# A mixture-of-experts kernel on Trainium2: the third row tile of each expert cut from 384 to 352 rows, with a branch at the end for the rows left out, and the last transfer freed of a wait

## The chip, the cores and the metric

The kernel runs on one core of a Trainium2 chip. The core has a matrix engine (PE, whose weight loads are shown apart as PEld), a vector engine (DVE), an activation engine (ACT), a general engine (POOL) and a queue engine (SP), each with an instruction stream of its own; they meet at semaphores. Transfers are started by SP, or by POOL where rows are scattered through a list of indices. The metric is the time of one execution on the device in microseconds, and lower is better.

## The reference

The input x has 8 sequences of 512 tokens with 256 features. Two layers follow each other, both with a residual: a causal attention with 16 heads whose context passes a convolution of width 3 and then attends again, and a block of attention with rotary embedding followed by a mixture of experts. The change concerns the mixture of experts. For the 4096 tokens (normalized rows `xf`) it computes

```python
probs = softmax(xf @ w_router)                 # 8 experts
topw, topi = top_k(probs, 2)                   # each token goes to two of them
combine = sum(one_hot(topi, 8) * (topw / sum(topw))[..., None], axis=1)
g = silu(einsum('td,xdh->txh', xf, wg))        # 256 -> 704, each expert
u = einsum('td,xdh->txh', xf, wu)
eo = einsum('txh,xhd->txd', g * u, wd)         # 704 -> 256
out = einsum('txd,tx->td', eo, combine)
```

All arithmetic is in f32. There are 4096 x 2 = 8192 pairs of a token and an expert, a mean of 1024 for each expert. How many an expert gets depends on the input.

## The kernel before

`block_kernel` calls `fast_path` and then, under a branch on the count `few`, `general_path`. The fast path assumes some bounds on its inputs, `sums_in_range` and `count` test them in the run itself, and the general path, which computes everything again without them, runs only where a test failed. In the traced run it is jumped over (L619).

The fast path has two stages. In the first, up to about 880 us, two attentions at a time go through a schedule written out turn by turn (`plan`, `units`). `route` picks the two experts of every token, and `slots` gives each pair a place in the table `xtab` in device memory. Expert `e` owns the `CAP` = 1152 rows from `e * CAP` on. `run` counts the places given so far and `limit` is the end of each expert's part. A row of the table holds the 256 features of the token, its number, and its eight weights. Rows that no token fills keep the padding that `fill` wrote at the start. Their token number lies outside the output, so that a transfer to it is dropped.

In the second stage every expert goes through its 1152 rows as three tiles of N = ET * P = 384. Of the 24 tiles, (0, 0) runs ahead, inside the end of the first stage; `places` lists the others: (0, 1), then experts 1 to 7 with their tiles 0 to 2, then (0, 2). `expert_tile` is a generator, and the loop at L1970 steps two tiles in turn, so that a tile's steps stand in this order on every engine:

- `load_rows` (L726, on SP) fetches the rows of the tile after next. Three buffers `xg` take turns, so a load waits until the scatters of the tile three before it have landed. `load_expert` (L711) fetches the weights of the next expert into one of two sets of buffers.
- Six transposes on PE (L744) and two scalings on ACT (L747) make `xgT`, with the features on the partitions. They stand ahead of the second product of the tile before.
- `up` (L755): for each of six blocks `k` of the hidden width the products with `wg` and `wu`, with the expert's weights stationary and the tile's 384 rows moving. ACT applies silu (L769, L772) and DVE multiplies (L770, L773) into `hT`. The last block is half as wide, and its two products share one.
- L780: for each `s` of three groups of 128 rows, six products with `hT` stationary and the 256 columns of `dn` (`wd`) moving. DVE multiplies by the token's weight for this expert into `share` (L787), and POOL scatters the rows of `share` with addition into `out` (L792).

The order on PE, ACT, DVE and POOL is the order in which the program issues (`manual_schedule`); only SP's is the framework's. In PSUM, `pgu` and `po` have two buffers each.

The scatters add to rows of `out` that others may also add to. `unordered` states what has to wait. Within a tile all rows are different, so its first two transfers wait only for the last transfer of the tile before (`added`) and for those that stored the residual (`stored`); the third also waits for the first two, so that to wait for it means to wait for all:

```python
for i in sent[:-1]:
    if last:
        tc.add_manual_dep(sent[-1], i.name, data, reason="the last one")
    else:
        tc.declare_no_dep(sent[-1], i, reason="rows of their own")
```

At n = 2 in the loop `sums_in_range` reduces the tests to a column `good` on DVE (L810 to L825), at n = 3 `count` sums it over the partitions with one product (L831) and writes `few` (L833). Every engine loads `few` at the end of its stream (L1986; SP earlier) and compares (L619). L2031 stands for the program's closing: SP waits for every semaphore, POOL drains, and the engines meet.

Of the kernel before, what the change touches and what calls it, by code (L numbers as in the profile page):

```python
# [11 lines left out]
F32 = mybir.dt.float32  # L12
I32 = mybir.dt.int32
AF = mybir.ActivationFunctionType
ALU = mybir.AluOpType
AX = mybir.AxisListType
PSUM = bass.MemoryType.PSUM

P = 128
B, S, D = 8, 512, 256  # L20
# [5 lines left out]
DC = D // P  # L26
# [11 lines left out]
NB = S // KB  # L38
LARGE = 1e20
ET = 3  # L40
CAP = 3 * ET * P
ROW = D + 1 + NE


# [566 lines left out]
@with_exitstack  # L611
def block_kernel(
    ctx: ExitStack,
    tc: tile.TileContext,
    *args: bass.AP,
):
    few = fast_path(tc, *args)

    with tc.If(few < P):  # L619
        general_path(tc, *args)  # L620


@with_exitstack
def fast_path(
    ctx: ExitStack,
    tc: tile.TileContext,
    x: bass.AP,
    wqkvT: bass.AP,
    bqkv: bass.AP,
# [49 lines left out]
            nc.sync.dma_start(xs[b], x[b * S : (b + 1) * S, :].rearrange("(c p) d -> p c d", p=P))  # L679


    dram = ctx.enter_context(tc.tile_pool(name="dram", bufs=1, space=bass.MemoryType.DRAM))
    xtab = dram.tile([NE * CAP, ROW], F32, tag="xtab", name="xtab")

    run = keep.tile([P, NE], F32, tag="run", name="run")
# [25 lines left out]
    def load_expert(e, gu, dn):  # L711
# [9 lines left out]
        nc.gpsimd.memset(dn[:TAIL, HT, :], 0.0)  # L721
        return e, gu, dn

    def load_rows(xg, e, i):
        r0 = e * CAP + i * N
        nc.sync.dma_start(xg, xtab[r0 : r0 + N, :].rearrange("(p s) w -> p s w", s=ET))  # L726
        return xg

    def token_of(xg, s):
        return bass.IndirectOffsetOnAxis(ap=xg[:, s, D : D + 1].bitcast(I32), axis=0)  # L730

    added = []

    stored = []

    def expert_tile(expert, xg, room):


        e, gu, dn = expert
        xgT = room("xgT")  # L740
        for d in range(DC):
            pt = room("pt")
            for s in range(ET):
                nc.tensor.transpose(  # L744
                    pt[:, s * P : (s + 1) * P], xg[:, s, d * P : (d + 1) * P], ident
                )
            nc.scalar.mul(xgT[:, d, :], pt, g2_sb[:, d : d + 1])  # L747
        yield
        hT = room("hT")
        nc.gpsimd.memset(hT[HT][:TAIL], 0.0)  # L750
        yield

        def up(ps, n0):
            for d in range(DC):
                nc.tensor.matmul(  # L755
                    ps,
                    gu[d][:, n0 : n0 + P],
                    xgT[:, d, :],
                    start=(d == 0),
                    stop=(d == DC - 1),  # L760
                )

        for k in range(NK):
            pg, pu = room("pgu")
            up(pg, k * P)
            sg = room("sg")
            if k < HT:
                up(pu, UP + k * P)
                nc.scalar.activation(sg, pg, AF.Silu)  # L769
                nc.vector.tensor_mul(hT[k], sg, pu)  # L770
            else:
                nc.scalar.activation(sg[TAIL:P, :], pg[:TAIL, :], AF.Silu)  # L772
                nc.vector.tensor_mul(hT[k][TAIL:P, :], sg[TAIL:P, :], pg[TAIL:P, :])  # L773
            yield
        sent = []
        share = room("share")
        for s in range(ET):
            po = room("po")
            for k in range(NK):
                nc.tensor.matmul(  # L780
                    po,
                    hT[k][:, s * P : (s + 1) * P],
                    dn[:, k, :],
                    start=(k == 0),
                    stop=(k == NK - 1),
                )
            nc.vector.tensor_scalar(  # L787
                share[:, s, :], po, xg[:, s, D + 1 + e : D + 2 + e], None, ALU.mult
            )

            sent.append(
                nc.gpsimd.indirect_dma_start(  # L792
                    out=out,
                    out_offset=token_of(xg, s),
                    in_=share[:, s, :],
                    in_offset=None,
                    bounds_check=B * S - 1,
                    oob_is_err=False,
                    compute_op=ALU.add,
                ).ins  # L800
            )
            unordered(sent, added[-1:] + stored, s == ET - 1)
            if s == ET - 1:
                added[:] = sent[-1:]
            yield


    def sums_in_range():
        good = keep.tile([P, 4], F32, tag="good", name="good")
        nc.vector.tensor_reduce(good[:, 0:2], total, AX.X, ALU.add)  # L810
        nc.vector.tensor_scalar(good[:, 0:2], good[:, 0:2], LARGE, None, ALU.is_lt)

        nc.vector.tensor_mul(good[:, 0:1], good[:, 0:1], turns[:, 1:2])
        nc.vector.tensor_mul(good[:, 1:2], good[:, 1:2], turns[:, 0:1])
        nc.vector.tensor_add(good[:, 0:1], good[:, 0:1], good[:, 1:2])
        nc.vector.tensor_reduce(good[:, 1:2], rtotal, AX.X, ALU.add)
        nc.vector.tensor_scalar(good[:, 1:2], good[:, 1:2], LARGE, None, ALU.is_lt)
        nc.vector.tensor_mul(good[:, 2:3], good[:, 0:1], good[:, 1:2])
        nc.vector.tensor_tensor(limit, run, limit, ALU.is_le)
        nc.vector.tensor_reduce(good[:, 3:4], limit, AX.X, ALU.min)  # L820
        nc.vector.tensor_mul(good[:, 2:3], good[:, 2:3], good[:, 3:4])

        nc.vector.tensor_tensor(early, early, needed, ALU.is_ge)
        nc.vector.tensor_reduce(good[:, 3:4], early, AX.X, ALU.min)
        nc.vector.tensor_mul(good[:, 2:3], good[:, 2:3], good[:, 3:4])  # L825
        return good

    def count(good, pc):
        all_one = keep.tile([P, 1], F32, tag="all_one", name="all_one")
        nc.vector.memset(all_one, 1.0)  # L830
        nc.tensor.matmul(pc[0:1, 0:1], good[:, 2:3], all_one, start=True, stop=True)  # L831
        few = keep.tile([1, 1], I32, tag="few", name="few")
        nc.vector.tensor_copy(few, pc[0:1, 0:1])  # L833
        return few

    with ExitStack() as att:
        wp = att.enter_context(tc.tile_pool(name="wp", bufs=1))
# [974 lines left out]
        with tc.manual_schedule(  # L1812
# [157 lines left out]
            for n, (e, i) in enumerate(places):  # L1970
                if i == 1 and n:
                    more = (e + 1) % NE
                    weights[more] = load_expert(more, *room("weights"))
                if n + 2 < len(places):
                    rows[n + 2] = load_rows(room("xg"), *places[n + 2])
                if n:
                    go_on(parts[n], 1 + NK)
                if n + 1 < len(places):
                    parts[n + 1] = expert_tile(weights[places[n + 1][0]], rows[n + 1], room)
                    go_on(parts[n + 1])  # L1980
                go_on(parts[n], ET)
                if n == 2:
                    good = sums_in_range()
                if n == 3:
                    few = count(good, room("po"))
    return nc.values_load(few, min_val=0, max_val=P)  # L1986


# [46 lines left out]
```

## Time and profile before

| | |
|---|---|
| three runs | 1419.48, 1420.53 (median), 1425.67 us |
| profiled execution | 1420.22 us |
| its span, from first to last instruction | 1418.5 us |
| granted PE clock, mean | 0.997 |
| expert products `pgu` (L755) | 1056 records, 345.8 us busy |
| second products `po` (L780) | 864 records, 190.6 us busy |
| scatters into `out` (L792) | 72, mean 1.555 us |
| first to last record of L755 | 848.2 to 1398.7 us |

The profile shows one execution. A product of f32 operands stands in it as two records, each with a weight load of its own: 22 products with `wg` and `wu` in a tile are 44 records, 18 with `wd` are 36. A transpose is one record. The records of PE overlap, so their mean duration (L755: 487 ns) is longer than the distance from one to the next, and a busy share near 100% only says that PE has no gap. What one more or one less record costs is read from the distances. The time of a run is longer than the span by what lies before the first instruction and after the last: 1.72 us in the profiled execution.

### The profile page before, as it was taken

The numbers are of one execution on the slowest core, as the hardware profiler recorded it, in microseconds if no ns is written. First come the engines' busy times: TensorE is split into PE (matmuls) and PEld (weight loads), VectorE is DVE, ScalarE is ACT, GpSimd is POOL, SyncE is SP. The second block draws the span as 40 slices with busy tenths as digits, with TensorE's granted clock in tenths as the row PEclk, the third lists the DMA queues.
The fourth block names the chain that finished last, engine by engine and source line by source line (L and its number), as shares of the span: only waits on it lengthen the run. The fifth ranks groups of instructions, "written<-read, shape, count | busy, mean of one in ns | idle before, by whom it ended". The sixth has DMA issues, their size and how long they took to land.

```text
span 1418.5 us, 31892 instructions
## 1 busy us (share of the span) xinstructions
PE 1375.9 (97%) x13476; PEld 893.0 (63%) x13476; DVE 740.7 (52%) x1466; ACT 725.4 (51%) x1175; POOL 526.5 (37%) x525
## 2 busy tenths in 40 slices
PE   8999999999999999999999999999999999999996
PEld 5566555566565665565565666676766767676674
DVE  5755887775977775976676855322121222222221
ACT  4777786776787775787776883211121111112110
POOL 3334333546334555434555344331212122221212
PEclk9999999999999999999999999999999999999998
DMA  5122122211001211011211022423232323232311
GB/s 150 59 85 86 62 81 77 77 43 54 13 32 46 88 43 43 13 56 43 86 64 67 24 79 88 115 46 95 32 94 39 90 43 89 38 90 64 69 22 14
DMA packets 65767, 88.68 MB, mean 63 GB/s; under 512 B 12880, under 2 KB 46096, under 8 KB 65616
## 3 DMA queue, kind: packets, MB, share of 16 engines
q1 hardware_dynamic: 52080, 69.21, 15.0%
q0 software_dynamic: 13536, 17.35, 7.0%
q8 instruction: 107, 1.75, 0.5%
q14 instruction: 44, 0.36, 0.1%
HBM read 36.62 MB, written 32.08 MB: 48 GB/s over the span
## 4 chain that ended last, share of the span: by engine, by line
PE 58%; DVE 5%; ACT 3%; issue 2%; DMA 1%; POOL 1%; POOLq 0%; DVEq 0%; ACTq 0%; SPq 0%
PE pgu L755 23%; PE po L780 12%; PE sc L1204 8%; PE av L1134 6%; PE mm L1044 4%; PE mm L1397 2%; ACT pr L1211 2%; PE mm L1033 1%; PE mm L1062 1%; DVE r L1164 1%; PE mm L744 1%; DVE c L1165 1%; PE mm L1286 1%; POOL out_dram L792 0%; DMA out_dram<-share,xg 0%
## 5 line engine op out<-in xcount | busy, mean ns | idle before, releaser
L1211 ACT ACTIVATE pr<-sc 128x1024 f32<-128x1024 f32 x432 | 418.7, 1023 | 143.8 <-PE sc L1204 141.4
L1219 POOL TENSOR_TENSOR pr<-pr,seen 128x512 f32<-128x512 f32 (+1 forms) x216 | 256.6, 1188 | 394.8 <-ACT pr L1211 385.5
L755 PE MATMUL pgu<-xgT,gu 128*128 128x384 f32 x1056 | 345.8, 487 | 2.2 <-DVE hT L770 1.6
L755 PEld LDWEIGHTS pgu<-xgT,gu 128*128 128x128 f32 x1056 | 200.0, 190 | 137.0 <-DVE hT L770 2.2
L769 ACT ACTIVATE sg<-pgu 128x384 f32<-128x384 f32 x120 | 58.8, 490 | 410.8 <-PE pgu L755 410.8
L792 POOL DMA_INDIRECT out_dram<-share,xg x72 | 112.0, 1555 | 385.8 <-DVE share L787 306.2
L1134 PE MATMUL av<-pr,va 64*32 64x64 f32 (+7 forms) x6144 | 218.8, 407 | 0.0
L770 DVE TENSOR_TENSOR hT<-sg,pgu 128x384 f32<-128x384 f32 x120 | 66.4, 554 | 247.2 <-ACT sg L769 247.2
L1204 PE MATMUL sc<-qT,kT 32*128 32x320 f32 (+7 forms) x2048 | 191.1, 434 | 4.3 <-ACT pr L1211 4.2
L780 PE MATMUL po<-dn,hT 128*128 128x256 f32 x864 | 190.6, 379 | 0.0
L1134 PEld LDWEIGHTS av<-pr,va 64*32 64x32 f32 x6144 | 113.1, 106 | 102.9 <-issue 73.9
L780 PEld LDWEIGHTS po<-dn,hT 128*128 128x128 f32 x864 | 162.4, 190 | 21.6
L1164 DVE RECIPROCAL r<-r 128x256 f32<-128x256 f32 x96 | 167.4, 1744 | 12.0 <-DMA r<-cs 11.9
L1204 PEld LDWEIGHTS sc<-qT,kT 32*128 32x128 f32 x2048 | 115.2, 184 | 77.5 <-ACT pr L1211 30.8
L787 DVE TENSOR_SCALAR share<-po,xg 128x256 f32<-128x256 f32 x72 | 34.8, 484 | 149.3 <-PE po L780 147.1
L1204 PE MATMUL sc<-q2T,kT 32*128 32x512 f32 (+7 forms) x1024 | 92.9, 434 | 0.6 <-ACT pr L1211 0.5
L1644 POOL DMA_INDIRECT xtab<-rows,slot x64 | 64.0, 1000 | 41.8 <-DVE pick L1633 26.3
L1204 PEld LDWEIGHTS sc<-q2T,kT 32*128 32x128 f32 x1024 | 58.3, 184 | 32.6 <-issue 14.7
L1044 PE MATMUL mm<-xT,wqkv_sb 128*128 128x512 f32 x128 | 62.7, 616 | 3.8 <-ACT mm L1539 2.3
L1044 PE MATMUL mm<-xaT,wqkv_sb 128*128 128x512 f32 x128 | 61.3, 612 | 2.0 <-DVE xaT L1292 2.0
L1397 PE MATMUL mm<-terms,conv_sb 128*128 128x256 f32 x256 | 62.7, 390 | 0.0
L1151 ACT ACTIVATE cs<-av 128x512 f32<-128x512 f32 x96 | 56.6, 603 | 4.5 <-PE av L1134 3.9
(177 smaller groups left out, 1302.5 us busy)
## 6 DMA issues: line engine op xcount, KB each, us to landing
r<-cs SPq DMA_DIRECT2D x96, 128.0 KB
xtab<-pad SPq DMA_DIRECT2D x24, 397.5 KB
xg<-xtab SPq DMA_DIRECT2D x24, 397.5 KB
gu<-in_wg_dram SPq DMA_DIRECT2D x18, 352.0 KB
cs<-cs SPq DMA_DIRECT2D x48, 128.0 KB
dn<-in_wd_dram SPq DMA_DIRECT2D x9, 640.0 KB
gu<-in_wu_dram SPq DMA_DIRECT2D x18, 320.0 KB
x<-in_x_dram SPq DMA_DIRECT2D x8, 512.0 KB
```

Of the source, the lines that this page charges most:

```text
L755: nc.tensor.matmul(ps, gu[d][:, n0 : n0 + P], xgT[:, d, :], start=(d == 0), stop=(d == DC - 1),)
L770: nc.vector.tensor_mul(hT[k], sg, pu)
L780: nc.tensor.matmul(po, hT[k][:, s * P : (s + 1) * P], dn[:, k, :], start=(k == 0), stop=(k == NK - 1),)
L792: nc.gpsimd.indirect_dma_start(out=out, out_offset=token_of(xg, s), in_=share[:, s, :], in_offset=None, bounds_check=B * S - 1, oob_is_err ...
L1044: nc.tensor.matmul(ps, w[:, d, n0 : n0 + P], srcT[:, d, :S], start=(d == 0), stop=(d == DC - 1),)
L1134: nc.tensor.matmul(av[i][g * HP : (g + 1) * HP, j * KB :], v[rows, j, ch * G + g, :], pr[rows, g, at : at + n], start=(j == 0), stop=(j == ...
L1164: nc.vector.reciprocal(r[:, half], r[:, half])
L1204: nc.tensor.matmul(sc[:, g - g0, at : at + S - j * KB], kT[r0 : r0 + HP, ch, j], qT[r0 : r0 + HP, ch, j * KB : S], start=True, stop=True,)
L1211: nc.scalar.activation(pr[:, g0 : g0 + 2], sc, AF.Exp, scale=SCALE)
L1219: nc.gpsimd.tensor_tensor(diag, diag, seen.unsqueeze(1).unsqueeze(1).to_broadcast([P, G, len(parts), KB]), ALU.mult,).ins
L1397: nc.tensor.matmul(ps[:, i], conv_sb[:, d, k, ch * P : (ch + 1) * P], self.terms[d][:, k], start=(d == 0), stop=(d == DC - 1),)
L1644: nc.gpsimd.indirect_dma_start(out=xtab, out_offset=bass.IndirectOffsetOnAxis(ap=slot[:, c, k : k + 1], axis=0), in_=rows[:, c, :], in_off ...
```

## The change

`MOST` = 1120 rows of each expert go through the fast path instead of `CAP` = 1152, so the tiles of an expert have 384, 384 and 352 rows; the table keeps its size. The third tile's rows are loaded in two transfers, 256 rows with two to a partition and 96 rows with one, where one transfer brought three to a partition. Its third group has 96 rows. The other tiles keep their shapes.

`rows_left` computes the last `FEW` = 32 rows of every expert from the table. It stands under a branch on a second count, which is 128 only if all tests hold with each `limit` lower by 32; `general_path` stands under a branch of its own inside that one. `sums_in_range` gets four more DVE operations, `count` returns two numbers (`held`), and the pools `dram` and `counts` are opened in `block_kernel`, around both.

The very last transfer of the last tile (`final`) is declared independent of the other two of its tile, where it waited for them.

```diff
@@ -38,7 +38,9 @@
 NB = S // KB
 LARGE = 1e20
 ET = 3
-CAP = 3 * ET * P
+FEW = 32
+MOST = 3 * ET * P - FEW
+CAP = MOST + FEW
 ROW = D + 1 + NE
 
 
@@ -614,16 +616,84 @@
     tc: tile.TileContext,
     *args: bass.AP,
 ):
-    few = fast_path(tc, *args)
-
-    with tc.If(few < P):
-        general_path(tc, *args)
+    dram = ctx.enter_context(tc.tile_pool(name="dram", bufs=1, space=bass.MemoryType.DRAM))
+    counts = ctx.enter_context(tc.tile_pool(name="counts", bufs=1))
+    xtab, seen = fast_path(tc, dram, counts, *args)
+
+
+    with tc.If(tc.nc.values_load(seen[:, 1:2], min_val=0, max_val=P) < P):
+        rows_left(tc, xtab, *args)
+        with tc.If(tc.nc.values_load(seen[:, 0:1], min_val=0, max_val=P) < P):
+            general_path(tc, *args)
+
+
+@with_exitstack
+def rows_left(ctx: ExitStack, tc: tile.TileContext, xtab: bass.AP, *args: bass.AP):
+
+    nc = tc.nc
+    wg, wu, wd, _, g2, _, _, out = args[-8:]
+    one = ctx.enter_context(tc.tile_pool(name="one", bufs=1))
+    pool = ctx.enter_context(tc.tile_pool(name="left", bufs=2))
+    ps = ctx.enter_context(tc.tile_pool(name="ps_left", bufs=2, space=PSUM))
+    ident = one.tile([P, P], F32, tag="ident", name="ident")
+    make_identity(nc, ident)
+    g_sb = one.tile([P, DC], F32, tag="g", name="g_sb")
+    nc.sync.dma_start(g_sb, g2)
+    for e in range(NE):
+        gu = pool.tile([P, DC, 2, HID], F32, tag="gu", name="gu")
+        for n, w in enumerate((wg, wu)):
+            nc.sync.dma_start(gu[:, :, n, :], w[e].rearrange("(c p) n -> p c n", p=P))
+        dn = pool.tile([P, NK, D], F32, tag="dn", name="dn")
+        nc.sync.dma_start(dn[:, :HT, :], wd[e, : HT * P, :].rearrange("(k p) d -> p k d", p=P))
+        nc.sync.dma_start(dn[:TAIL, HT, :], wd[e, HT * P :, :])
+        xg = pool.tile([FEW, ROW], F32, tag="xg", name="xg")
+        nc.sync.dma_start(xg, xtab[e * CAP + MOST : (e + 1) * CAP, :])
+        xgT = pool.tile([P, DC, FEW], F32, tag="xgT", name="xgT")
+        for d in range(DC):
+            pt = ps.tile([P, FEW], F32, tag="pt", name="pt")
+            nc.tensor.transpose(pt, xg[:, d * P : (d + 1) * P], ident[:FEW, :FEW])
+            nc.scalar.mul(xgT[:, d, :], pt, g_sb[:, d : d + 1])
+        hT = pool.tile([P, NK, FEW], F32, tag="hT", name="hT")
+        for k in range(NK):
+            m = min(P, HID - k * P)
+            pgu = ps.tile([P, 2, FEW], F32, tag="pgu", name="pgu")
+            for n in range(2):
+                for d in range(DC):
+                    nc.tensor.matmul(
+                        pgu[:m, n, :],
+                        gu[:, d, n, k * P : k * P + m],
+                        xgT[:, d, :],
+                        start=(d == 0),
+                        stop=(d == DC - 1),
+                    )
+            sg = pool.tile([P, FEW], F32, tag="sg", name="sg")
+            nc.scalar.activation(sg[:m], pgu[:m, 0, :], AF.Silu)
+            nc.vector.tensor_mul(hT[:m, k, :], sg[:m], pgu[:m, 1, :])
+        po = ps.tile([FEW, D], F32, tag="po", name="po")
+        for k in range(NK):
+            m = min(P, HID - k * P)
+            nc.tensor.matmul(
+                po, hT[:m, k, :], dn[:m, k, :], start=(k == 0), stop=(k == NK - 1)
+            )
+        share = pool.tile([FEW, D], F32, tag="share", name="share")
+        nc.vector.tensor_scalar(share, po, xg[:, D + 1 + e : D + 2 + e], None, ALU.mult)
+        nc.gpsimd.indirect_dma_start(
+            out=out,
+            out_offset=bass.IndirectOffsetOnAxis(ap=xg[:, D : D + 1].bitcast(I32), axis=0),
+            in_=share,
+            in_offset=None,
+            bounds_check=B * S - 1,
+            oob_is_err=False,
+            compute_op=ALU.add,
+        )
 
 
 @with_exitstack
 def fast_path(
     ctx: ExitStack,
     tc: tile.TileContext,
+    dram: tile.TilePool,
+    counts: tile.TilePool,
     x: bass.AP,
     wqkvT: bass.AP,
     bqkv: bass.AP,
@@ -679,7 +749,6 @@
             nc.sync.dma_start(xs[b], x[b * S : (b + 1) * S, :].rearrange("(c p) d -> p c d", p=P))
 
 
-    dram = ctx.enter_context(tc.tile_pool(name="dram", bufs=1, space=bass.MemoryType.DRAM))
     xtab = dram.tile([NE * CAP, ROW], F32, tag="xtab", name="xtab")
 
     run = keep.tile([P, NE], F32, tag="run", name="run")
@@ -721,32 +790,43 @@
         nc.gpsimd.memset(dn[:TAIL, HT, :], 0.0)
         return e, gu, dn
 
+    def rows_of(i):
+        return min(N, MOST - i * N)
+
     def load_rows(xg, e, i):
         r0 = e * CAP + i * N
-        nc.sync.dma_start(xg, xtab[r0 : r0 + N, :].rearrange("(p s) w -> p s w", s=ET))
-        return xg
-
-    def token_of(xg, s):
-        return bass.IndirectOffsetOnAxis(ap=xg[:, s, D : D + 1].bitcast(I32), axis=0)
+        n = rows_of(i)
+        s, m = divmod(n, P)
+        nc.sync.dma_start(
+            xg[:, :s, :], xtab[r0 : r0 + s * P, :].rearrange("(p s) w -> p s w", s=s)
+        )
+        if m:
+            nc.sync.dma_start(xg[:m, s, :], xtab[r0 + s * P : r0 + n, :])
+        return xg, n
+
+    def token_of(xg, s, m):
+        return bass.IndirectOffsetOnAxis(ap=xg[:m, s, D : D + 1].bitcast(I32), axis=0)
 
     added = []
 
     stored = []
 
-    def expert_tile(expert, xg, room):
+    def expert_tile(expert, rows, room, final=False):
 
 
         e, gu, dn = expert
-        xgT = room("xgT")
+        xg, n = rows
+        size = [min(P, n - s * P) for s in range(ET)]
+        xgT = room("xgT")[:, :, :n]
         for d in range(DC):
-            pt = room("pt")
-            for s in range(ET):
+            pt = room("pt")[:, :n]
+            for s, m in enumerate(size):
                 nc.tensor.transpose(
-                    pt[:, s * P : (s + 1) * P], xg[:, s, d * P : (d + 1) * P], ident
+                    pt[:, s * P : s * P + m], xg[:m, s, d * P : (d + 1) * P], ident[:m, :m]
                 )
             nc.scalar.mul(xgT[:, d, :], pt, g2_sb[:, d : d + 1])
         yield
-        hT = room("hT")
+        hT = [t[:, :n] for t in room("hT")]
         nc.gpsimd.memset(hT[HT][:TAIL], 0.0)
         yield
 
@@ -761,9 +841,9 @@
                 )
 
         for k in range(NK):
-            pg, pu = room("pgu")
+            pg, pu = (t[:, :n] for t in room("pgu"))
             up(pg, k * P)
-            sg = room("sg")
+            sg = room("sg")[:, :n]
             if k < HT:
                 up(pu, UP + k * P)
                 nc.scalar.activation(sg, pg, AF.Silu)
@@ -774,32 +854,32 @@
             yield
         sent = []
         share = room("share")
-        for s in range(ET):
-            po = room("po")
+        for s, m in enumerate(size):
+            po = room("po")[:m]
             for k in range(NK):
                 nc.tensor.matmul(
                     po,
-                    hT[k][:, s * P : (s + 1) * P],
+                    hT[k][:, s * P : s * P + m],
                     dn[:, k, :],
                     start=(k == 0),
                     stop=(k == NK - 1),
                 )
             nc.vector.tensor_scalar(
-                share[:, s, :], po, xg[:, s, D + 1 + e : D + 2 + e], None, ALU.mult
+                share[:m, s, :], po, xg[:m, s, D + 1 + e : D + 2 + e], None, ALU.mult
             )
 
             sent.append(
                 nc.gpsimd.indirect_dma_start(
                     out=out,
-                    out_offset=token_of(xg, s),
-                    in_=share[:, s, :],
+                    out_offset=token_of(xg, s, m),
+                    in_=share[:m, s, :],
                     in_offset=None,
                     bounds_check=B * S - 1,
                     oob_is_err=False,
                     compute_op=ALU.add,
                 ).ins
             )
-            unordered(sent, added[-1:] + stored, s == ET - 1)
+            unordered(sent, added[-1:] + stored, s == ET - 1 and not final)
             if s == ET - 1:
                 added[:] = sent[-1:]
             yield
@@ -816,22 +896,28 @@
         nc.vector.tensor_reduce(good[:, 1:2], rtotal, AX.X, ALU.add)
         nc.vector.tensor_scalar(good[:, 1:2], good[:, 1:2], LARGE, None, ALU.is_lt)
         nc.vector.tensor_mul(good[:, 2:3], good[:, 0:1], good[:, 1:2])
-        nc.vector.tensor_tensor(limit, run, limit, ALU.is_le)
-        nc.vector.tensor_reduce(good[:, 3:4], limit, AX.X, ALU.min)
+        ok = keep.tile([P, NE], F32, tag="ok", name="ok")
+        nc.vector.tensor_tensor(ok, run, limit, ALU.is_le)
+        nc.vector.tensor_reduce(good[:, 3:4], ok, AX.X, ALU.min)
         nc.vector.tensor_mul(good[:, 2:3], good[:, 2:3], good[:, 3:4])
 
         nc.vector.tensor_tensor(early, early, needed, ALU.is_ge)
         nc.vector.tensor_reduce(good[:, 3:4], early, AX.X, ALU.min)
         nc.vector.tensor_mul(good[:, 2:3], good[:, 2:3], good[:, 3:4])
+
+        nc.vector.tensor_scalar(limit, limit, -float(FEW), None, ALU.add)
+        nc.vector.tensor_tensor(ok, run, limit, ALU.is_le)
+        nc.vector.tensor_reduce(good[:, 3:4], ok, AX.X, ALU.min)
+        nc.vector.tensor_mul(good[:, 3:4], good[:, 2:3], good[:, 3:4])
         return good
 
     def count(good, pc):
         all_one = keep.tile([P, 1], F32, tag="all_one", name="all_one")
         nc.vector.memset(all_one, 1.0)
-        nc.tensor.matmul(pc[0:1, 0:1], good[:, 2:3], all_one, start=True, stop=True)
-        few = keep.tile([1, 1], I32, tag="few", name="few")
-        nc.vector.tensor_copy(few, pc[0:1, 0:1])
-        return few
+        nc.tensor.matmul(pc[0:1, 0:2], all_one, good[:, 2:4], start=True, stop=True)
+        held = counts.tile([1, 2], I32, tag="held", name="held")
+        nc.vector.tensor_copy(held, pc[0:1, 0:2])
+        return held
 
     with ExitStack() as att:
         wp = att.enter_context(tc.tile_pool(name="wp", bufs=1))
@@ -1976,14 +2062,16 @@
                 if n:
                     go_on(parts[n], 1 + NK)
                 if n + 1 < len(places):
-                    parts[n + 1] = expert_tile(weights[places[n + 1][0]], rows[n + 1], room)
+                    parts[n + 1] = expert_tile(
+                        weights[places[n + 1][0]], rows[n + 1], room, n + 2 == len(places)
+                    )
                     go_on(parts[n + 1])
                 go_on(parts[n], ET)
                 if n == 2:
                     good = sums_in_range()
                 if n == 3:
-                    few = count(good, room("po"))
-    return nc.values_load(few, min_val=0, max_val=P)
+                    held = count(good, room("po"))
+    return xtab, held
 
 
 # ---- launch: one core; inputs and outputs as the reference has them ----
```

## The prediction

> **What bounds the kernel now.** I read the busy shares first, then the stages, then the chain that ended last, then the timeline of the end.
>
> ```profile
> PE 1375.9 (97%) x13476; PEld 893.0 (63%) x13476; DVE 740.7 (52%) x1466; ACT 725.4 (51%) x1175; POOL 526.5 (37%) x525
> ...
> 960.00:980.00 20.00, 19.40 (x79) 13.66 (x78) 4.34 (x10) 3.00 (x6) 3.49 (x3) 1.00 0.45 120
> ...
> 1020.00:1406.00 386.00, 386.00 (x1468) 270.05 (x1467) 81.74 (x154) 66.68 (x134) 88.99 (x75) 1.00 0.28 60
> ```
>
> The last two lines are stages (columns: PE, PEld, DVE, ACT, POOL, granted clock, DMA share, GB/s). From 900 to 1406.9 us only the experts run, and PE idles once, 0.60 us, at L831. DVE, ACT and POOL are busy for about a fifth of it, the granted clock is 1.00. A PE microsecond removed here is a microsecond of the span, as long as nothing else is late.
>
> The chain of waits prices a tile (columns: start, us, what):
>
> ```profile
> 1362.34 14.19 PE pgu L755 x44
> 1376.53 0.65 PE mm L744 x6
> 1377.19 7.77 PE po L780 x36
> ...
> 1405.13 3.72 DMA out_dram<-share,xg
> 1408.86 0.03 POOLq L792
> 1408.88 0.51 issue
> 1409.39 0.50 POOLq L1986
> 1409.89 1.25 POOL out_dram L792
> ```
>
> A tile is 44 records of 384 columns (14.19/44 = 322.5 ns each), 36 of 256 (7.77/36 = 215.8 ns) and 6 transposes of 128 (about 109 ns). The slope is (322.5 - 215.8)/128 = 0.833 ns for a column. The last lines are the end: the last transfer waits until the one before it has landed.
>
> ```profile
> 1404.37 0.48 DVE L787 TENSOR_SCALAR share<-po,xg 128x256 f32<-128x256 f32 x1 [2.11 <-PE po L780]
> 1405.13 1.55 POOL L792 DMA_INDIRECT out_dram<-share,xg  x1 [1.03 <-DVE share L787]
> 1406.96 0.48 DVE L787 TENSOR_SCALAR share<-po,xg 128x256 f32<-128x256 f32 x1 [2.10 <-PE po L780]
> 1409.60 1.55 POOL L792 DMA_INDIRECT out_dram<-share,xg  x1 [2.92 <-DMA out_dram<-share,xg]
> ```
>
> Its input is ready at 1407.44, it starts at 1409.60. What follows it, from the answers for L619 and L2031 (columns: min/median/max ns, start):
>
> ```profile
> L619 POOLq EVENT_SEMAPHORE  x2: 17/30/43, 1412.8 to 1412.9; - x2
> ...
> L619 POOLq COMPARE_BRANCH  x1: 53/53/53, 1410.0 to 1410.0; - x1
> ...
> L619 POOLq INC_SWDGE_SEM  x1: 1057/1057/1057, 1413.0 to 1413.0; - x1
> ...
> L2031 POOLq DRAIN  x3: 46/103/3580, 1414.1 to 1418.2; - x3
> ```
>
> POOL branches at 1409.96, runs its next instruction at 1412.78, increments DMA semaphores (1.06 us), drains (3.58 us), and the span ends at 1418.5.
>
> [...] The chain shows that price, 3.72 us from issue to landing. [...] the trace has 53 ns for the record but 2.82 us until POOL's next instruction.
>
> **The change part by part.** Sums are against the profiled execution: 1420.22 us, 1.72 of it outside the span of 1418.5. It is 0.31 below the median of three runs.
>
> *Eight tiles of 352 rows.* All eight third tiles start after 945 us, where PE is full. L755: 44 records x 32 columns x 0.833 ns = 1.173 us a tile, 9.38 in all. L744: two of six transposes 32 columns narrower, 2 x 26.7 ns x 8 = 0.43. L780 streams dn, still 256 columns: nothing. PE: **-9.81**.
>
> *Shorter ACT, DVE and POOL work* (scalings, silu, products, memset at 352): these idle and PE waits for none of them; nothing.
>
> *Row loads in two.* Eight more DMAs on SP, about 0.33 us of issue each. What is queued behind: weights and later rows. The last row load was issued at 1346.1 and first read at 1376.4, 30 us later; landing is some us. Slack falls by about a microsecond: nothing. If that cover went, each of eight tiles would stall PE by its lateness.
>
> *Four more small DVE operations before `good`.* Rows of the same kind take 0.15 to 0.20 us, 0.7 in sum. Behind them is the first hT of the tile at 954, which was ready 0.25 us after `good`. It slips some 0.45 us and ends near 958.4; PE needs its pgu buffer at 954.08 + 2 x 2.37 = 958.8. Nothing, at worst 0.5 us once.
>
> *`count` with operands swapped* (two columns for one): the 0.60 us stall on `all_one` stays.
>
> *Last transfer without its wait.* It may start 0.28 us after its share (as the one before: 1404.85 to 1405.13), at 1407.72 on the old clock, 1.88 earlier. POOL's branch moves with it and POOL resumes at 1410.90. What is late next: in the built program the skipped branch makes POOL itself wait for all eight DMA semaphores, the last transfer's too, where SP did that before. Four more semaphore instructions at 0.07 us bring 1411.25; the landing, 3.72 after issue, 1411.44. So the increment starts at about 1411.5 instead of 1412.98: **-1.5**; at best -1.75, if 96 rows land sooner.
>
> *Increment of eight semaphores instead of three.* No row shows that. Lower bound 0, if its time is fixed (or under it, if the drain overlaps it); upper bound in proportion: 1.057 x 8/3 - 1.057 = +1.76. The smallest POOL instructions, memsets of one column (L923), take 0.12 us, so a fixed part exists but need not be large, and no row decides: I take the middle, **+0.8**. The drain behind it stays at 3.58, because what it flushes is not shown to depend on the count; its bound is in the rivals.
>
> *The branch.* `held` is read where `few` was, one compare in each engine. The reference's routing on its inputs gives the experts 988, 1016, 996, 1027, 1048, 1113, 1052 and 952 rows. None is over 1120, so rows_left is jumped over as general_path was, with one far jump as before: nothing.
>
> Sum: -9.81 - 1.5 + 0.8 = -10.5, a span of 1408.0 and 1409.7 us; 1410.0 against the median, which lies 0.31 higher.
>
> **The rivals.** *The end gives its gain back*: the increment costs in proportion: -9.81 - 1.5 + 1.76 = -9.55, 1411.0 by the median. If the drain too goes by semaphores, 3.58 x 5/3 = 5.97 more: 1416.9. For it: POOL's end is serial, nothing covers it, and the work handed to it grows from three to eight. Against: a part of each instruction is fixed. 16%, a quarter of it with the drain.
>
> *Another stage takes the bound*: the second half of xg, or hT, holds PE back in each third tile. From 1.2 us a tile the gain on PE is gone and 1420.53 - 1.5 + 0.8 = 1419.8 is left. Against: 30 us of slack for rows and, in the loop, over 2 us of DVE idling between hT products. With it the case that a 352-column record doesn't cost 0.833 ns a column less; L1204 has 480 ns for 320 columns and 533 for 384, the same slope. 8%.
>
> *Slower: the branch is taken.* It decides as soon as one expert has more than 1120 rows. Then rows_left reads every expert's weights again: 2.16 MB x 8 = 17.3 MB. The fastest slice of DMA in the expert stage moved 155 GB/s: 112 us, so some 1521. The margin is 7 rows at expert 5, and the kernel's own sums would have to route 8 near ties otherwise. 3%.
>
> **How the numbers follow.** Forecast 73%, rivals 16, 8 and 3. The range: from 1410.0 down by the 0.8, by 0.25 for an earlier landing, by 1.06 for a drain that overlaps the old increment too, and by a spread of 1 us below the median (1419.48): 1406.9. Up: 1411.0 and 2 us of spread, since one of three runs was 5 us over: 1413.0. Outside stay the second and third rival, the longer drain and some of the spread. A measurement here can tell about 0.5% (7.1 us) from no change, a limit of 1413.4: faster 0.85 (forecast and first rival, less the longer drain), same 0.12, slower 0.03.
>
> **What would show it.** L755 with 352 columns at 460 ns (486 less 26.7) in 352 records, about 295.8 ns apart; a tile of 352 at 21.39 us against 22.62; PE full to about 1397; the last transfer 0.28 us after its share; POOL's increment 4.6 us after PE's last matmul instead of 6.1. Wrong would be: idle PE ahead of L744 or L755 in third tiles, an increment of over 2.8 us, a longer drain, any instruction of rows_left.

## The result and the profile after

The changed kernel takes **1411.27 us** (median of five runs, 1408.44 to 1413.80), the kernel before 1420.53 on the same chip (median of five, 1419.48 to 1425.67). The ratio is 0.9928, 95% interval 0.9909 to 0.9948. The forecast was 1410.0. The profiled execution took 1413.67 us, its span is 1411.9, its mean granted clock 0.994; in the profile before these were 1420.22, 1418.5 and 0.997.

The busy shares of the page after, and two stages of it (columns PE, PEld, DVE, ACT, POOL, granted clock, DMA share, GB/s):

```profile
PE 1369.0 (97%) x13476; PEld 892.3 (63%) x13476; DVE 739.6 (52%) x1470; ACT 723.6 (51%) x1175; POOL 525.2 (37%) x525
...
960.00:980.00 20.00, 19.94 (x81) 14.16 (x79) 5.78 (x22) 3.82 (x8) 5.06 (x4) 1.00 0.40 107
1020.00:1401.00 381.00, 381.00 (x1483) 270.71 (x1482) 80.80 (x155) 65.22 (x134) 89.66 (x75) 1.00 0.28 61
```

PE has the same 13476 records and no gap from 1020 us on, where DVE and ACT are busy for the same share as before (21 and 17%); the 5.78 us of DVE between 960 and 980, before 4.34, hold tests that lay ahead of 960 before. PE still bounds the expert stage, so what its records got shorter is what the stage got shorter.

The groups of instructions from 900 to 1395 us, shapes kept apart (busy us, mean ns of one, then idle time ahead):

```profile
L835 PE MATMUL pgu<-xgT,gu 128*128 128x384 f32 x630 | 206.0, 486 | 0.0
...
L860 PE MATMUL po<-dn,hT 128*128 128x256 f32 x714 | 158.1, 379 | 0.0
...
L835 PE MATMUL pgu<-xgT,gu 128*128 128x352 f32 x352 | 105.4, 459 | 0.0
...
L860 PE MATMUL po<-dn,hT 128*96 128x256 f32 x84 | 19.3, 379 | 0.0
```

352 records of 352 columns, 459 ns each, stand beside those of 384 with 486. The second products (L860, before L780) take 379 ns whether 128 or 96 rows are stationary; their weight loads take 190 and 163 ns, less than the 216 ns from one record to the next.

The chain of waits (start, us, what), over the last tiles:

```profile
1336.84 14.19 PE pgu L835 x44
1351.03 0.61 PE mm L824 x6
1351.64 7.80 PE po L860 x36
1359.44 13.02 PE pgu L835 x44
...
1393.88 7.78 PE po L860 x36
1401.66 0.03 issue
1401.68 0.49 DVE share L867
1402.18 0.03 issue
1402.21 0.50 POOLq L624
1402.71 1.16 POOL out_dram L872
```

A tile of 352 has its 44 records in 13.02 us where one of 384 has 14.19, and behind PE's last record the landing of an earlier transfer is gone from the chain. The timeline of the end shows the last transfer right behind its `share`, while the one before it, which lands 3.9 us after its start, is still under way:

```profile
1399.86 1.55 POOL L872 DMA_INDIRECT out_dram<-share,xg  x1 [1.03 <-DVE share L867]
1401.68 0.48 DVE L867 TENSOR_SCALAR share<-po,xg 96x256 f32<-96x256 f32 x1 [2.11 <-PE po L860]
1402.44 1.43 POOL L872 DMA_INDIRECT out_dram<-share,xg  x1 [1.03 <-DVE share L867]
```

What POOL does then, with ACT and DVE for comparison, from the answers for L624 (before L619) and L2119 (before L2031; count, min/median/max ns, start of first and last):

```profile
L624 POOLq EVENT_SEMAPHORE  x6: 17/30/43, 1406.0 to 1406.4; - x6
L624 ACTq EVENT_SEMAPHORE  x2: 17/17/17, 1396.9 to 1397.0; - x2
...
L624 DVEq EVENT_SEMAPHORE  x2: 21/21/21, 1405.8 to 1405.9; - x2
...
L624 ACTq COMPARE_BRANCH  x1: 50/50/50, 1394.4 to 1394.4; - x1
...
L624 DVEq COMPARE_BRANCH  x1: 72/72/72, 1402.6 to 1402.6; - x1
L624 POOLq COMPARE_BRANCH  x1: 53/53/53, 1402.8 to 1402.8; - x1
L624 POOLq INC_SWDGE_SEM  x1: 1045/1045/1045, 1406.5 to 1406.5; - x1
...
L2119 POOLq DRAIN  x3: 50/103/3539, 1407.6 to 1411.7; - x3
```

Eight semaphores are incremented in 1.045 us; three took 1.057. The drain takes 3.54 where it took 3.58. From the branch to POOL's next instruction it is 3.19 us. The obvious suspect, the last transfer's landing, isn't what POOL waits for there: the transfer landed 3.1 us after its start, at 1405.56, 0.41 us before that instruction. And ACT, which branches 8 us before that transfer starts, also stands still for 2.43 us behind its branch (DVE for 3.25).

The two spans can't be subtracted as they stand. In the profile after, the first stage has two stretches at half the granted clock, which the profile before has not:

```profile
475.60:479.00 3.40, 1.44 (x44) 0.71 (x36) 3.33 (x7) 2.96 (x6) 1.07 (x2) 1.00 0.11 40
479.00:482.40 3.40, 2.52 (x12) 2.11 (x16) 1.95 (x4) 0.13 (x2) 1.55 (x2) 0.50 0.32 121
482.40:485.80 3.40, 3.40 (x19) 1.71 (x12) 3.28 (x4) 1.84 (x2) 0.00 (x0) 0.50 0.09 34
...
881.80:885.20 3.40, 1.74 (x11) 1.23 (x11) 1.56 (x5) 1.02 (x2) 1.02 (x2) 1.00 0.47 87
885.20:888.60 3.40, 3.40 (x24) 1.97 (x23) 0.29 (x1) 1.41 (x3) 0.95 (x1) 0.50 0.34 116
```

They last 6.83 and 3.41 us; at half clock up to half of that is lost, by estimate 5.1 us. So PE ends at 1401.65 and not near 1397, though the expert stage is as forecast. By the mean clocks (0.992 to 0.998 over the executions of before), such stretches come and go from one execution to the next in both kernels: executions of after with a mean clock of 0.997 have spans of 1406.7 and 1407.9, those with 0.994 have 1411.9 and 1412.1. What the change did is therefore taken below from the stages, and the medians bear it out within some 2 us.

### The profile page after: what moved, and what is told of

The parts are those of the page before. It is cut to its first block, busy times and chain, and to the rows that moved or that the text cites. A ratio compares the mean times of both kernels' runs of the same rounds, so it can differ in the third digit from the quotient of the medians.

```text
span 1411.9 us, 31919 instructions
## 1 busy us (share of the span) xinstructions
PE 1369.0 (97%) x13476; PEld 892.3 (63%) x13476; DVE 739.6 (52%) x1470; ACT 723.6 (51%) x1175; POOL 525.2 (37%) x525
## 4 chain that ended last, share of the span: by engine, by line
PE 59%; DVE 5%; ACT 4%; DMA 1%; issue 1%; POOL 1%; DVEq 0%; POOLq 0%; ACTq 0%; SPq 0%
PE pgu L835 23%; PE po L860 13%; PE sc L1290 8%; PE av L1220 5%; PE mm L1130 3%; ACT pr L1297 2%; PE mm L1483 2%; PE mm L1119 1%; PE mm L1148 1%; PE mm L824 1%; DVE r L1250 1%; DVE c L1251 1%; PE mm L1372 1%; DMA r<-cs 1%; DMA cs<-cs 0%
## 5 line engine op out<-in xcount | busy, mean ns | idle before, releaser
L835 PE MATMUL pgu<-xgT,gu 128*128 128x384 f32 (+1 forms) x1056 | 337.0, 478 | 1.9 <-DVE hT L850 1.6
L835 PEld LDWEIGHTS pgu<-xgT,gu 128*128 128x128 f32 x1056 | 200.4, 190 | 128.3 <-DVE hT L850 2.2
L849 ACT ACTIVATE sg<-pgu 128x384 f32<-128x384 f32 (+1 forms) x120 | 57.7, 481 | 404.5 <-PE pgu L835 404.4
L1220 PE MATMUL av<-pr,va 64*32 64x512 f32 (+7 forms) x6144 | 216.3, 407 | 0.0
L850 DVE TENSOR_TENSOR hT<-sg,pgu 128x384 f32<-128x384 f32 (+1 forms) x120 | 65.0, 543 | 240.3 <-ACT sg L849 240.3
L860 PE MATMUL po<-dn,hT 128*128 128x256 f32 (+1 forms) x864 | 190.8, 379 | 0.0
L860 PEld LDWEIGHTS po<-dn,hT 128*128 128x128 f32 (+1 forms) x864 | 159.9, 187 | 23.9
L1250 DVE RECIPROCAL r<-r 128x256 f32<-128x256 f32 x96 | 167.4, 1744 | 11.8 <-DMA r<-cs 11.7
L867 DVE TENSOR_SCALAR share<-po,xg 128x256 f32<-128x256 f32 (+1 forms) x72 | 34.8, 483 | 148.6 <-PE po L860 148.5
```

The lines of the kernel that those rows point to most:

```text
L835: nc.tensor.matmul(ps, gu[d][:, n0 : n0 + P], xgT[:, d, :], start=(d == 0), stop=(d == DC - 1),)
L860: nc.tensor.matmul(po, hT[k][:, s * P : s * P + m], dn[:, k, :], start=(k == 0), stop=(k == NK - 1),)
L1220: nc.tensor.matmul(av[i][g * HP : (g + 1) * HP, j * KB :], v[rows, j, ch * G + g, :], pr[rows, g, at : at + n], start=(j == 0), stop=(j == ...
L1250: nc.vector.reciprocal(r[:, half], r[:, half])
```

## The experiments

Four kernels ran on one chip (before: 1422.41 there): the tiles alone, the transfer alone, the wait put back, and 64 rows. The other four ran on a second (before: 1423.12). Ratios are against the kernel before on the same chip.

### The tiles of 352 alone

The transfer's wait is kept, and `rows_left` with its branch is left out:

```diff
-    with tc.If(tc.nc.values_load(seen[:, 1:2], min_val=0, max_val=P) < P):
-        rows_left(tc, xtab, *args)
-        with tc.If(tc.nc.values_load(seen[:, 0:1], min_val=0, max_val=P) < P):
-            general_path(tc, *args)
+    with tc.If(tc.nc.values_load(seen[:, 0:1], min_val=0, max_val=P) < P):
+        general_path(tc, *args)
@@
-            unordered(sent, added[-1:] + stored, s == ET - 1 and not final)
+            unordered(sent, added[-1:] + stored, s == ET - 1)
```

> The tiles of 352 rows alone: the last transfer keeps its wait and rows_left with its branch is left out (an expert's rows beyond 1120 would be dropped; on these inputs there are none). Theory (PE pays 0.833 ns a column, the end is a separate term): records of 352 columns 295.8 ns apart, 9.8 us less PE time, and from PE's last matmul to the end of the span 11.6 us as before. So about 9.8 us below the kernel before where the granted clock is the same. Rival (the two gains are not separate, the end loses what the tiles gain): less than 8 us.

Measured: 1415.68 us, ratio 0.9945 (0.9913 to 0.9976). Its profiled execution took 1410.85 with the clock at 0.997 and no half-clock stretch, as in the profile before: PE ends at 1397.33 where it ended at 1406.92, **9.59 us earlier**. The timeline of its end and the chain's line ahead of the transfer:

```profile
1397.37 0.48 DVE L865 TENSOR_SCALAR share<-po,xg 96x256 f32<-96x256 f32 x1 [2.11 <-PE po L858]
1399.95 1.43 POOL L870 DMA_INDIRECT out_dram<-share,xg  x1 [2.87 <-DMA out_dram<-share,xg]
```

```profile
1395.54 3.65 DMA out_dram<-share,xg
```

With the wait the transfer starts 2.6 us after PE's end, as before. From PE's end to the end of the span it is 11.57 us, as before, so the tiles' part of the gain all comes from PE. The median is only 6.7 us below the kernel before, less than the 8 us that the rival allows; but three of the five executions had mean clocks of 0.993 to 0.996, and the two at 0.997 (1410.85 and 1411.42) lie 9.7 and 9.1 us below the median of the six executions of the kernel before with that clock on this chip (1420.52).

### The last transfer alone

The kernel before, with its last tile called as `final`:

```diff
-            unordered(sent, added[-1:] + stored, s == ET - 1)
+            unordered(sent, added[-1:] + stored, s == ET - 1 and not final)
```

> The kernel before with the last transfer freed of its wait, nothing else. Theory: POOL starts it 0.28 us after its share, 1.9 us earlier, and POOL's branch and all behind it move with it: 9.7 us from PE's last matmul to the end instead of 11.6. Three semaphores are incremented as before, in 1.06 us. Rival (a landing becomes the new wait of the end): SP waits for the last transfer, and the drain or SP's waits end last, less than 1 us gained.

Measured: 1420.74 us (15 runs), ratio 0.9993 (0.9978 to 1.0007). The times can't show a gain of 1.6 us here; the trace does. Timeline, and the answers for L619 and L2033:

```profile
1410.75 1.55 POOL L792 DMA_INDIRECT out_dram<-share,xg  x1 [1.04 <-DVE share L787]
```

```profile
L619 POOLq COMPARE_BRANCH  x1: 53/53/53, 1411.1 to 1411.1; - x1
...
L619 POOLq INC_SWDGE_SEM  x1: 1057/1057/1057, 1414.4 to 1414.4; - x1
...
L2033 POOLq DRAIN  x3: 46/103/3580, 1415.5 to 1419.6; - x3
```

From PE's last record to the end of the span it is 9.96 us instead of 11.57. The transfer starts 1.88 earlier and 0.3 of that is lost between the branch and POOL's next instruction, 3.14 us where it was 2.82.

### The change with the wait put back

The edit of the last transfer's experiment reversed, in the changed kernel.

> The changed kernel with the last transfer's wait put back. Theory: the last transfer starts some 2.2 us after its share again; POOL, which in the skipped branch waits for that landing too, begins its increment of eight semaphores only then: 12 us from PE's last matmul to the end, 0.4 more than before, 1.7 more than in the changed kernel. The increment takes 1.05 us, for eight as for three. Rival (the increment goes by the number of semaphores): over 2 us in this kernel too.

Measured: 1414.17 us, ratio 0.9937 (0.9908 to 0.9967). From PE's end to the end of the span it is 11.61 us, where 12 was expected. The timeline and the answers for L624:

```profile
1403.50 1.43 POOL L872 DMA_INDIRECT out_dram<-share,xg  x1 [2.91 <-DMA out_dram<-share,xg]
```

```profile
L624 POOLq EVENT_SEMAPHORE  x6: 17/30/43, 1406.5 to 1406.9; - x6
...
L624 POOLq INC_SWDGE_SEM  x1: 1041/1041/1041, 1407.0 to 1407.0; - x1
```

Eight semaphores again cost what three do: 1.041 us. POOL was past all its six semaphores 3.4 us after the transfer's issue, without standing still at one, so the landing is not what holds the increment. The branch took 2.61 us here; the wait's removal is worth 11.61 - 10.30 = 1.3 us in the changed kernel. Against the tiles alone (11.57), which lack `rows_left` and its branch, this kernel loses 0.04 us at the end. So in these two profiles the added branch costs next to nothing where it isn't taken: its semaphores take 0.33 us more, and POOL's next instruction comes 0.33 us sooner (2.61 for 2.94).

### No branch at all

`block_kernel` ends with the fast path, so `rows_left` and the general path are gone and the tests are not read:

```diff
-    with tc.If(tc.nc.values_load(seen[:, 1:2], min_val=0, max_val=P) < P):
-        rows_left(tc, xtab, *args)
-        with tc.If(tc.nc.values_load(seen[:, 0:1], min_val=0, max_val=P) < P):
-            general_path(tc, *args)
```

> The changed kernel without any branch at its end: rows_left and general_path are left out, the tests are computed and not read. Theory (the end is a serial chain on POOL: branch, about 3 us until its next instruction, half a microsecond of semaphores, 1.05 us of increment, then the drain): without the branch the drain starts when the last transfer is issued or landed, so the end is 10.3 us minus 3.2 to 4.7, that is 5.6 to 7 us from PE's last matmul. Rival (the drain waits for the scatter's landing and its own time only, and the branch lies beside it): over 9 us.

Measured: 1411.13 us, ratio 0.9904 (0.9879 to 0.9929), profiled at a clock of 0.994. From PE's end to the end of the span it is 6.55 us, against 10.30 with the branch: **the jump with what belongs to it, semaphores and increment included, costs 3.75 us** on the path. The timeline, and the answers for L2115:

```profile
1404.36 1.43 POOL L868 DMA_INDIRECT out_dram<-share,xg  x1 [1.03 <-DVE share L863]
```

```profile
L2115 POOLq DRAIN  x3: 46/97/5207, 1404.1 to 1409.8; - x3
```

The longest drain is issued at 1404.12, already ahead of the last transfer's record, and ends at 1409.33. That is some 3.55 us after the transfer's record (1404.36 + 1.43 = 1405.79), much as it ends 3.57 us after the increment in the changed kernel. So here it doesn't wait for the branch or the increment, but runs behind POOL's last instruction, whichever it is. Not all of the 3.75 us need show in the time: in two of the four executions here the part of the time outside the span is 2.9 and 3.5 us, where it is 1.7 to 2.0 in the other two.

### 64 rows left, and the branch taken

```diff
-FEW = 32
+FEW = 64
```

Expert 5 has 1113 rows, so 25 of them lie beyond 1088 and `rows_left` runs.

> The changed kernel with FEW = 64, so that third tiles have 320 rows and expert 5, with 1113 rows, has 25 beyond 1088: the branch is taken. Theory (my price of the slower rival): PE ends the experts another 9.8 us earlier, then rows_left reads 17.3 MB of weights and costs about 112 us at 155 GB/s, so 100 us or more over the kernel before. Rival: PE sets its pace, 8 experts x about 11 us of products with 32 to 64 rows, 88 us, or the serial chain of one expert (load, transpose, products, scatter) with little overlap, 150 us or more.

Measured: 1514.11 us (1503.39 to 1521.87), ratio 1.0649 (1.0592 to 1.0706). The experts' PE work ends at 1395.13 in a span of 1501.6. With an end of 10.3 us behind it the span would be 1405.4, so the branch taken costs about 96 us in this execution, the fastest of four. Its stages (columns as above):

```profile
1400.00:1420.00 20.00, 13.43 (x57) 11.32 (x58) 1.31 (x6) 1.85 (x8) 0.00 (x0) 0.51 0.54 177
1420.00:1440.00 20.00, 19.14 (x130) 14.14 (x128) 3.73 (x15) 3.70 (x16) 2.88 (x2) 0.98 0.67 224
1440.00:1460.00 20.00, 17.91 (x127) 13.76 (x127) 3.92 (x15) 4.14 (x18) 3.51 (x3) 1.00 0.74 238
```

Once it runs, DMA moves up to 238 GB/s and PE is busy for 90 to 96% of a slice at full clock. After 11 us until its first product it takes some 10.6 us an expert: 9.0 to 9.8 us for the six at full clock, in which PE stands idle for at most 0.7 us until the expert's rows are there, and 15.4 and 13.8 us for the two that fall into stretches of half clock. So PE sets most of the pace, as the rival of this run has it, and not the weights: 155 GB/s was only what the expert stage had asked for. The median of this run is 10.7 us above the profiled execution, its clocks reach down to 0.973; it is 92 us over the kernel before, where 100 or more was expected.

The run also showed something that no price by columns holds: its tiles of 320 rows save only 1.46 us each (three tiles in a row take 66.39 us and took 67.85), where 44 records with 64 columns less at 0.833 ns make 2.35 us and the narrower transposes 0.1 more. So PE ends the experts 2.2 us ahead of the tiles of 352 alone (1397.33), and not 9.8 as expected. The timeline of one:

```profile
1364.83 1.24 PE L835 MATMUL pgu<-xgT,gu 128*128 128x320 f32 x4
...
1365.90 1.16 PE L824 MATMUL mm<-ident,xg 128*128 128x128 f32 x6
...
1366.99 8.18 PE L860 MATMUL po<-dn,hT 128*128 128x256 f32 x36
1375.11 12.11 PE L835 MATMUL pgu<-xgT,gu 128*128 128x320 f32 x44
1387.05 8.08 PE L860 MATMUL po<-dn,hT 128*128 128x256 f32 x36
```

From the first transpose (1365.90) to the first `po` (1366.99) it is 1.09 us, where after has 0.61. The form changes six times in a tile, between 128\*128 and one with 64 rows: four times at the transposes (64\*128) and twice at the last group of `po` (128\*64). At each change the next record starts some 94 ns late, and the one after it another 50 to 104 ns; that makes the missing 1 us, some 0.16 us for each change in this trace. Groups of 96 and 90 rows show no such pause; `po` takes 0.02 to 0.03 us longer in their tiles.

### 38 rows left

`FEW = 38` leaves 1114 rows to the fast path, one more than expert 5 has. The size is fitted to these inputs; with others the branch would be taken sooner.

> The changed kernel with FEW = 38: third tiles of 346 rows, one more than expert 5 fills, the branch still not taken on these inputs. Theory (PE pays by the column): 6 columns x 0.833 ns x 46 records x 8 tiles = 1.8 us less PE time than with 352, records of 346 columns 290.8 ns apart, the same end of 10.3 us. Rival (a width that is no multiple of 32 costs extra): records further apart than 295.8 ns and no gain.

Measured: 1410.37 us, ratio 0.9907 (0.9884 to 0.9929). The groups by shape from 900 to 1395 us:

```profile
L835 PE MATMUL pgu<-xgT,gu 128*128 128x346 f32 x352 | 103.7, 454 | 0.0
...
L860 PE MATMUL po<-dn,hT 128*90 128x256 f32 x84 | 19.3, 379 | 0.0
```

The records stand 290.8 ns apart, 5.0 less than those of 352 columns: six columns at 0.833. The slope holds for a size that is no multiple of 32 too. The end is 10.28 us.

### PE filled ahead of a half-clock stretch

Twelve transposes of `ident` (1.3 us) in the gap of PE ahead of the stretch at 885 us, in the changed kernel; their result is not used:

```diff
+            ps = mm_tile()
+            for i in range(12):
+                nc.tensor.transpose(ps[:, i % NC * P : (i % NC + 1) * P], ident, ident)
             t.transpose3(0)
```

> The changed kernel with 12 transposes of the identity (1.3 us) on PE, where it waits for DVE's rows at about 882 us. Theory (the scatter of the runs comes from stretches of 3.4 us at half the granted clock, which follow stretches in which PE was busy for about half of the time): no half-clock stretch begins between 880 and 890 us, while those near 423 and 479 us stay possible; so no run loses those 1.7 us, and the median falls by 0 to 1.5 us, the fastest runs stay where they are (1408.4). Rival (the stretches come at random): they are there as before, or the filling costs 1.3 us in each run.

Measured: 1413.10 us, ratio 0.9921 (0.9901 to 0.9941). The timeline:

```profile
878.28 5.34 PE L860 MATMUL po<-dn,hT 128*128 128x256 f32 x24
883.46 1.47 PE L2041 MATMUL mm<-ident 128*128 128x128 f32 x12
885.05 1.46 PE L1372 MATMUL mm<-ident,rows 128*128 128x128 f32 x8
```

The filling fits into the gap and delays nothing: from the `po` ahead of the gap to the transposes behind it it is 6.77 us, as in the profile of the changed kernel. No half clock follows near 885 in this profile, but there are stretches at 213.5 and 851.8, and the time is that of the changed kernel within its interval. **Inconclusive**: of the profiles without the filling four in eight have a half-clock stretch near 885, of the two with it none has. That is too few, and no time is shown to be gained.

### 38 rows and the filling

Both edits together, the version that the runs pointed to.

> Both: FEW = 38 and the 12 transposes at 882 us. If the theories of both hold: 1.8 us below the filled kernel, with the fastest runs at about 1406.6 us, below both kernels of the case. If the filling only delays: no better than FEW = 38 alone.

Measured: 1409.59 us, ratio 0.9899 (0.9876 to 0.9921). It has the lowest ratio of all, but its interval overlaps those of 38 rows alone and of the change, and its fastest execution (1407.76) is no faster than that of 38 rows alone (1407.08). It beats the kernel before; that it beats the changed kernel, or that the filling adds anything to the 38 rows, is not shown.

## Why the prediction was right, step by step

**Eight tiles of 352 rows, -9.81: right, 0.3 too large.** Records of 352 columns stand 295.8 ns apart and a tile's 44 take 13.02 us, as forecast. Two small terms were off: the 96-wide transposes stand 86.6 ns apart (82.5 forecast, so 0.07 us less gain in all), and `po` takes 7.80 us and not 7.77 in these tiles (7.796 against 7.772, 0.19 in eight). That leaves 9.55; the tiles alone, profiled at the same clock, gave 9.59.

**Nothing from rows, ACT and DVE: right.** PE has no gap ahead of a third tile, and the idle time ahead of L835 is 0.0 in the groups above. The four more DVE operations ended with `good` at 962.06 and the `hT` behind them at 962.49, 0.6 us before PE needed its buffer (958.33 + 2 x 2.37 = 963.06). The stall at `count` is as long as before, 0.60 us.

**Last transfer without its wait, -1.5: the start right, what follows mis-sized.** It starts 0.80 us after PE's last record instead of 2.68, so 1.88 earlier, as forecast. But POOL needed 3.19 us from the branch to its next instruction, not 2.82: 0.37 given back. The semaphores took 0.53 us where the forecast had 0.35 (before: 0.20). The landing, which the forecast took for the last to be waited for, was not it: it came at 1405.56, 3.1 us after the start and not 3.7, before POOL reached its semaphores, and with and without the wait POOL passed them without standing still. The increment started 4.85 us after PE's end; 4.6 was forecast, 6.06 was before.

**Increment of eight semaphores, +0.8: wrong, it is 0.** 1.045 and 1.041 us for eight, 1.057 and 1.047 for three. The middle between two bounds was taken because no row decided; the lower bound was the truth, and the rival that "the end gives its gain back" falls with it. From PE's end to the end of the span it is 10.30 us, 1.27 less than before, where -1.5 + 0.8 = -0.7 was forecast: the end gave 0.6 more than expected, and PE 0.3 less.

**The sum.** -9.55 - 1.27 = -10.8 at equal clock, -10.5 forecast. That it comes so close is in part luck: the increment's 0.8 us that isn't there, and 0.3 us each of gain too much from PE and from the last transfer, mostly cancel. The median moved by 9.3; what is missing fits the clock: the two executions of after with a mean clock of 0.997 (1408.44 and 1409.59 us) lie 11.8 and 10.6 us below the profiled one of before with the same clock (1420.22). The forecast allowed for them only as a spread of 1 us down and 2 us up.

**The branch, and the rival of it: nothing where it isn't taken, and that is what the trace shows:** no instruction of `rows_left`. Taken it costs 96 us in the profiled execution, not 112; the step that failed is the bound: not the weights at 155 GB/s set the pace but PE, at 9.0 us an expert where the clock is full.

**Another stage taking the bound** didn't happen: PE is busy for all of the 381 us from 1020 on.

## What to carry to other kernels

Where PE has no gap, price a smaller tile by the distance between its records and the slope of two sizes; it came true here to 3% over eight tiles, but look for a change of the tile form first, which took back 1 of 2.4 us in tiles whose last group had 64 rows. A wait removed at the very end is worth only what the chain behind it leaves: 1.88 us of an earlier start became 1.3, and the jump over code that is never run, with its semaphores and the increment, still costs 3.75. When the clock varies from one execution to the next, compare stages and the distances in them, and read a median as the sum of the change and the clock.

## What the runs showed of the hardware

- After the jump over code that isn't run POOL's next instruction comes 2.6 to 3.2 us later. It isn't the landing of the last transfer that it waits for (in the changed kernel that came 0.41 us before). The delay is 2.82, 2.94 and 2.61 us in the three profiles with the transfer's wait (before, tiles alone, wait put back), in which DVE takes its own branch 2.1 us before POOL, and 3.14, 3.19, 3.17, 3.21 and 3.17 us in the five without it (transfer alone, the change, 38 rows, the filling, both), in which DVE's branch is only 0.2 us ahead. So the longer delay goes with the removal of the wait; why stays open.
- The increment of DMA semaphores on this path takes 1.04 to 1.06 us, for three or for eight (1.19 in the run with 64 rows, where the branch is taken). The closing drain ends 3.55 to 3.61 us after POOL's last instruction, even where it was issued before that one had begun; in the run with 64 rows it takes 4.11.
- The granted clock fell to one half for 3.41 us, or twice that, after 3.4 us in which PE was busy for 1.44 or 1.74 us. No busy share is shown at which the clock falls: over all profiles 13 stretches of 3.41 or 6.83 us follow 3.41 us with 0.68 to 2.56 us of PE's work, while in the profile before PE is busy for only 1.64 us from 878.50 to 881.91 and the clock stays full. That these stretches make the spread of the times fits the mean clocks; that filling PE prevents them is not shown.
